# Self-attention in three float32r products: rows of v's two forms 320 floats apart, and the projection's tiles in the attention's buffers

## The chip, the cores and the metric

The kernel runs on one core of a Trainium2 chip. The metric is the device time of one execution in microseconds (us), the median of three runs. The engines are TensorE (PE; its weight loads are listed apart as PEld), VectorE (DVE), ScalarE (ACT), GpSimd (POOL) and SyncE (SP), which issues transfers.

## The reference, cut to what matters

```python
# x: (4, 64, 64, 256) float32; Wq, Wk: (256, 128); Wv: (256, 256); gamma: (1,)
q = einsum('bwhc,cd->bwhd', x, Wq) + bq          # N = 64*64 = 4096
k = einsum('bwhc,cd->bwhd', x, Wk) + bk
v = einsum('bwhc,cd->bwhd', x, Wv) + bv
pq, pk, pv = (t.reshape(B, -1, N) for t in (q, k, v))   # (4, 128, N), (4, 128, N), (4, 256, N)
energy = einsum('bcn,bcm->bnm', pq, pk)
attention = softmax(energy, axis=-1)
out = einsum('bcm,bnm->bcn', pv, attention)
return gamma * out.reshape(x.shape) + x
```

Four images, each with 4096 x 4096 energies over a depth of 128, and a sum over them with 256 rows of v.

## The kernel before: the parts that are touched

[...] The kernel therefore splits each operand into forms and adds up three products: for the energies two into `sa` and one into `sb`, for the attention `h` with `vh` and `l` with `vl` into one sum and `d` with `vd` into another. An image is handled in 16 groups of 256 queries; a group has 8 steps of 512 keys (4 tiles of 128). In each step TensorE does 12 energy products and 24 attention products. In a product the first operand named below is the stationary one, of 128 x 128, loaded as weights; the second one streams past, 256 or 258 columns of it. Two extra columns of ones in `vh` and `vl` give the sums that softmax divides by.

```python
NB = 256; NJ = NB // P; NG = N // NB; NU = NM // 4; STEPS = NG * NU; LOOK = 3
VC = C + 4                                   # floats in a row of vh and vl: 260
# ... pools in order of place:
xpool, xtpool, qkv = pool("xpool", 3), pool("xtpool", 3), pool("qkv", 1)
pool("pad", 1).tile([P, 16], F32, name="pad")
ppool = pool("ppool", 2)
pool("pad2", 1).tile([P, 112], F32, name="pad2")
work, kpool = pool("work", 2), pool("kpool", 3)
# ...
vh = qkv.tile([P, NM, VC], F32R, tag="vh", name="vh")
vl = qkv.tile([P, NM, VC], F32R, tag="vl", name="vl")
vd = qkv.tile([P, NM, C], F32R, tag="vd", name="vd")
# ... energies of half a step:
for i in range(2):
    for to, f, first, last in ((sa, 0, True, False), (sa, 1, False, True), (sb, 2, True, True)):
        nc.tensor.matmul(to[:, i], kt[:, 2 * k + i, f, :], q[:, f], start=first, stop=last)
# ... attention products of a step; h, l and d are ppool tiles [P, 4, NB]:
for left, right in ((h, vh), (l, vl), (d, vd)):
    for j in range(NJ):
        out_ = bb[:, j, :] if left is d else acc[j]
        for i in range(4):
            m = 2 * t + i // 2 + NI * (i % 2)
            nc.tensor.matmul(
                out_, left[:, i, j * P : (j + 1) * P], right[:, m, : out_.shape[1]],
                # ... start, stop
            )
```

Before an image's attention comes its projection, 16 iterations of 256 tokens: x is transposed, and TensorE computes q and k (`qk`) and v; q and the forms of k go to DRAM and come back tile by tile. The energies of the first steps are mixed into its last iterations (`begin`), and the first tiles of the next image are projected within the last steps of an image.

```python
def qk_out(i):
    now["qk"] = work.tile([P, 2, 2 * C2], F32, tag="qk", name=f"qks_{b}_{i}")
    return ((now["qk"], 0),)
def v_out(i):
    now["v4"] = work.tile([P, KC, C], F32, tag="v4", name=f"v4_{b}_{i}")
    return now["v4"], bv4_sb, 1.0 / E
# ... in project_qk:
f = kpool.tile([P, 2, 3, P], F32R, tag="f", name=f"f_{b}_{i}", bufs=2)
halved(f, x[:, :, C2:])
nc.gpsimd.dma_start(kf[b, i // 2][:, i % 2], f.rearrange("p s j d -> p s (j d)"))
# ...
def load_q(b, g):
    t = work.tile([P, NJ, P], F32, tag="qr", name=f"qr_{b}_{g}", bufs=1)
    nc.sync.dma_start(t, qd[b, g])
    loads[b, "qr", g] = t
# ... the loop of an image's steps, cut:
for u in range(STEPS):
    # ... energies of step u + 3; join and upper (x*y and h) of step u + 2
    halves(b, u + 1)          # l and d of the next step
    attend(b, u)
    # ... at a group's end: whole, finish (scale, transpose, add x, store)
```

Of the kernel before, what the change touches and what calls it, by code (L numbers as in the profile page):

```python
# [9 lines left out]
F32 = mybir.dt.float32  # L10
F32R = mybir.dt.float32r
# [9 lines left out]
def kernel(  # L21
# [37 lines left out]
    B, W, H, C = x.shape  # L59
    P = 128  # L60
    N = W * H
    C2 = C // 2
    NM = N // P
    KC = C // P
# [10 lines left out]
    XB = 256  # L75
# [98 lines left out]
    NB = 256  # L174
    NJ = NB // P
# [1 line left out]
    NU = NM // 4  # L177
    STEPS = NG * NU
    LOOK = 3
    VC = C + 4  # L180
    E = 2.0**-12


# [15 lines left out]
    with ExitStack() as fast:  # L199
        fast.enter_context(tc.manual_schedule())  # L200
        pool = lambda name, bufs, **kw: fast.enter_context(
            tc.tile_pool(name=name, bufs=bufs, **kw)
        )
        xpool, xtpool, qkv = pool("xpool", 3), pool("xtpool", 3), pool("qkv", 1)

        pool("pad", 1).tile([P, 16], F32, name="pad")
        ppool = pool("ppool", 2)
        pool("pad2", 1).tile([P, 112], F32, name="pad2")
        work, kpool = pool("work", 2), pool("kpool", 3)
        dram = pool("dram", 2, space=DRAM)  # L210
        ps_s = pool("ps_s", 2, space=PSUM)
# [3 lines left out]
# [4 lines that stand above are left out]
# [3 lines left out]
        images, qd, kf, units, loads, now = [], {}, {}, {}, {}, {}  # L222
# [14 lines left out]
        def image(b):  # L237
            def xt_out(i):
                return xtpool.tile([P, KC, 2, P], F32, tag="xt", name=f"xts_{b}_{i}")

            def qk_out(i):
                now["qk"] = work.tile([P, 2, 2 * C2], F32, tag="qk", name=f"qks_{b}_{i}")
                return ((now["qk"], 0),)

            def v_out(i):
                now["v4"] = work.tile([P, KC, C], F32, tag="v4", name=f"v4_{b}_{i}")
                return now["v4"], bv4_sb, 1.0 / E

            images.append(Projection(b, xpool, lambda: next(now["banks"]), xt_out, qk_out, v_out))

            for g in range(NG):
                qd[b, g] = dram.tile([P, NJ, P], F32, tag=f"qd{g}", name=f"qd_{b}_{g}")
            for t in range(NU):
                kf[b, t] = dram.tile([P, 2, 2, 3 * P], F32R, tag=f"kf{t}", name=f"kf_{b}_{t}")

        def halved(f, x):

            h = f[:, :, 0, :]
            nc.scalar.activation(h, x, AF.Identity, scale=UPPER / 64)
            for j, s, op in ((1, -64.0, ALU.add), (2, 64.0 * (1.0 + E), ALU.subtract)):  # L260
                nc.vector.scalar_tensor_tensor(
                    f[:, :, j, :], h.bitcast(F32), s, x, ALU.mult, op
                )

        def project_qk(b, i):
            images[b].qk(i)
            x = now["qk"]
            for s in range(2):
                nc.gpsimd.dma_start(qd[b, i // 2 + NG // 2 * s][:, i % 2, :], x[:, s, :C2])
            f = kpool.tile([P, 2, 3, P], F32R, tag="f", name=f"f_{b}_{i}", bufs=2)  # L270
            halved(f, x[:, :, C2:])
            nc.gpsimd.dma_start(kf[b, i // 2][:, i % 2], f.rearrange("p s j d -> p s (j d)"))

# [15 lines left out]
                )  # L289

        def load_q(b, g):
            t = work.tile([P, NJ, P], F32, tag="qr", name=f"qr_{b}_{g}", bufs=1)
            nc.sync.dma_start(t, qd[b, g])
            loads[b, "qr", g] = t

        def halve_q(b, g):
            t = work.tile([P, 3, NJ, P], F32R, tag="q", name=f"q_{b}_{g}")
            halved(t.rearrange("p f j d -> p j f d"), loads.pop((b, "qr", g)))
            loads[b, "q", g] = t

        def load_k(b, u):
            if u < STEPS:
                t = kpool.tile([P, 4, 3, P], F32R, tag="k", name=f"k_{b}_{u}")
                nc.gpsimd.dma_start(t.rearrange("p (i s) f d -> p i s (f d)", s=2), kf[b, u % NU])  # L304
                loads[b, "k", u] = t

        def energy(b, u, k):

            g, t = divmod(u, NU)
            if k == 0:  # L310
                x = ppool.tile([P, 4, NB], F32, tag="x", name=f"x_{b}_{u}", bufs=3)
                y = ppool.tile([P, 4, NB], F32, tag="y", name=f"y_{b}_{u}")
                units[b, u] = x, y
            x, y = units[b, u]
            q, kt = loads[b, "q", g], loads[b, "k", u]
            sa = ps_s.tile([P, 2, NJ, P], F32, tag="a", name=f"sa_{b}_{u}_{k}")
            sb = ps_s.tile([P, 2, NJ, P], F32, tag="b", name=f"sb_{b}_{u}_{k}")
# [3 lines that stand above are left out]
                        to[:, i], kt[:, 2 * k + i, f, :], q[:, f], start=first, stop=last  # L321
                    )
            for to, sp, scale in ((x, sa, (1.0 + E) / E), (y, sb, -1.0 / E)):
                nc.scalar.activation(  # L324
                    to[:, 2 * k : 2 * k + 2, :],
                    sp.rearrange("p i j d -> p i (j d)"),
                    AF.Exp,
                    scale=scale,
                )

        def join(b, u):

            x, y = units[b, u]
            nc.vector.tensor_tensor(x, x, y, ALU.mult)  # L334
            units[b, u] = x

        def upper(b, u):
            h = ppool.tile([P, 4, NB], F32R, tag="h", name=f"h_{b}_{u}", bufs=3)
            nc.scalar.activation(h, units[b, u], AF.Identity, scale=UPPER)  # L339
            units[b, u] = units[b, u], h  # L340
# [123 lines left out]

        def begin(b, i):

            if i == 5:
                load_q(b, 0)
            if i == 9:
                halve_q(b, 0)  # L470
            if i in (4, 6, 8):
                load_k(b, i // 2 - 2)
            if i >= 10:
                energy(b, (i - 10) // 2, i % 2)
            if i in (12, 14):
                join(b, i // 2 - 6)
            if i in (13, 15):
                upper(b, i // 2 - 6)
                load_k(b, i // 2 - 3)

        image(0)
        for b in range(B):
            pr = images[b]
            if b == 0:
                now["banks"] = energies
                pr.transposed(0)
                pr.transposed(1)
                project_qk(b, 0)
            for i in range(1, NI):
                if i == 3:  # L490
                    now["banks"] = outputs
                if i + 1 < NI:
                    pr.transposed(i + 1)
                while i == 1 and active:
                    proceed()
                begin(b, i)
                project_qk(b, i)
                if i == NI - 1:
                    halves(b, 0)
                project_v(b, i - 1)  # L500
                proceed()
            project_v(b, NI - 1)
            for u in range(STEPS):
                g, t = divmod(u, NU)
                ahead = u + LOOK
                if ahead // NU + 1 < NG and ahead % NU == 3:
                    load_q(b, ahead // NU + 1)
# [32 lines left out]
            if b + 1 < B:  # L540
                images[b + 1].transposed(1)
                project_qk(b + 1, 0)

    NB = 512
    NG = N // NB
    NJ = NB // P
    NP = NM // 2
    xg, og = columns(x, NB), columns(out, NB)
    with tc.If(nc.values_load(again[0:1, 0:1]) > 0), ExitStack() as general:
        pool = lambda name, bufs, **kw: general.enter_context(  # L550
            tc.tile_pool(name=name, bufs=bufs, **kw)
        )
        xpool, xtpool, qkv = pool("gx", 2), pool("gxt", 2), pool("gqkv", 1)
        ppool, work = pool("gp", NP + 2), pool("gw", 1)
# [3 lines left out]
        for b in range(B):  # L558
# [16 lines left out]
            for g in range(NG):  # L575
                ps = []
                mx = work.tile([P, 2, NB], F32, tag="mx", name=f"gmx_{b}_{g}")
                for t in range(NP):
# [9 lines left out]
                    p = ppool.tile([P, 2, NB], F32, tag="p", name=f"gp_{b}_{g}_{t}")  # L588
# [89 lines left out]
```

## Time and profile before

| | before |
|---|---|
| time, median of 3 runs | 2481.36 us (2479.54 to 2482.91) |
| span of the profiled execution | 2476.8 us |
| TensorE busy | 2463.2 us (99%), 19,982 records |
| weight loads busy | 2419.1 us (98%) |
| VectorE / ScalarE / GpSimd busy | 2103.2 (85%) / 1807.9 (73%) / 424.4 us (17%) |
| granted TensorE clock | 0.999 |
| energy products `sa`, `sb` | 4096 and 2048 |
| attention products h, l, d | 4096 each |
| projection products `qk`, `v` (records) | 512 each, 121.3 and 120.3 us busy |

A line of the costliest groups reads: line, engine, operation, output <- inputs, shape, count, then busy time and the mean of one in ns, then the idle time of the engine before them and who ended it. Two of VectorE's and one of ScalarE's:

```profile
L334 DVE TENSOR_TENSOR x<-x,y 128x1024 f32<-128x1024 f32 x512 | 625.8, 1222 | 144.2 <-ACT y L324 144.2
L345 DVE TENSOR_TENSOR l<-x,h 128x1024 fp32r<-128x1024 f32 x512 | 624.2, 1219 | 0.0
L339 ACT ACTIVATE h<-x 128x1024 fp32r<-128x1024 f32 x512 | 543.6, 1062 | 46.3 <-DVE x L334 38.4
```

Products overlap in TensorE's pipeline, so the duration of one (276 ns and more) is over twice the distance between the starts of two; the time is made by that distance. The last part of the page has the transfers, with the median time from issue to landing:

```profile
x<-in_x_dram SPq DMA_DIRECT2D x128, 256.0 KB, 4.3
kf<-f POOLq DMA_DIRECT2D x64, 384.0 KB, 3.7
...
qd<-qks POOLq DMA_DIRECT2D x128, 64.0 KB, 3.1
qr<-qd SPq DMA_DIRECT2D x64, 128.0 KB, 3.0
```

### The profile page before, as it was taken

The page shows a single profiled execution, that of the slowest core. Times are in us where ns is not written, and L with a number is a line of the kernel's source. Part 1 is how long each engine was busy: PE and PEld are TensorE (multiplying, and loading weights), DVE is VectorE, ACT ScalarE, POOL GpSimd, SP SyncE. Part 2 cuts the span into 40 slices and gives each one's busy share as a digit, 9 for nine tenths or more (in the row PEclk, how much of TensorE's full clock was granted, in tenths as well). Part 3 has the DMA queues.
Part 4 walks back from the last instruction along what each step waited for, and adds up shares of the span by engine and source line. Part 5 has one row for each costly group of instructions (what it writes and reads, how often), then busy time and mean ns, then how long its engine had stood idle before and what let it go on. Part 6 is the DMA issues. An engine that isn't in the chain of part 4 may idle for free.

```text
span 2476.8 us, 50085 instructions
## 1 busy us (share of the span) xinstructions
PE 2463.2 (99%) x19982; PEld 2419.1 (98%) x19982; DVE 2103.2 (85%) x2440; ACT 1807.9 (73%) x3138; POOL 424.4 (17%) x780
## 2 busy tenths in 40 slices
PE   9999999999999999999999999999999999999998
PEld 8999999999899999999989999999998999999998
DVE  5888888888698888888869888888886988888887
ACT  5777777777677777777667777777766777777775
POOL 4211111111411111111141111111114111111110
PEclk9999999999999999999999999999999999999999
DMA  7766666674766666666477666666647666666663
GB/s 235 218 194 213 202 206 200 196 217 150 236 215 195 207 202 207 203 193 215 138 239 224 199 195 209 205 209 196 199 146 247 219 202 198 204 204 209 200 201 110
DMA packets 137408, 498.92 MB, mean 201 GB/s; under 512 B 15536, under 2 KB 57264, under 8 KB 137168
## 3 DMA queue, kind: packets, MB, share of 16 engines
q0 software_dynamic: 92320, 453.17, 58.4%
q1 hardware_dynamic: 44304, 42.22, 5.7%
q8 instruction: 160, 2.62, 0.4%
q14 instruction: 80, 0.66, 0.1%
q10 hardware_dynamic: 544, 0.26, 0.0%
HBM read 445.25 MB, written 50.33 MB: 200 GB/s over the span
## 4 chain that ended last, share of the span: by engine, by line
PE 95%; ACT 2%; DVE 1%; issue 1%; DMA 1%; POOL 0%; SPq 0%; ACTq 0%; DVEq 0%; POOLq 0%
PE a L370 39%; PE bb L370 19%; PE sa L320 18%; PE sb L320 10%; PE qk L136 4%; PE v L157 4%; PE ot L416 1%; PE xt L123 1%; ACT h L339 1%; DVE x L334 1%; ACT x L324 0%; ACT y L324 0%; ACT vh L284 0%; DVE vd L287 0%; DMA kf<-f 0%
## 5 line engine op out<-in xcount | busy, mean ns | idle before, releaser
L324 ACT ACTIVATE x<-sa 128x512 f32<-128x512 f32 x1024 | 607.5, 593 | 381.0 <-PE sa L320 334.9
L334 DVE TENSOR_TENSOR x<-x,y 128x1024 f32<-128x1024 f32 x512 | 625.8, 1222 | 144.2 <-ACT y L324 144.2
L320 PE MATMUL sa<-q,k 128*128 128x256 f32 x4096 | 740.2, 279 | 1.2 <-ACT x L324 1.1
L345 DVE TENSOR_TENSOR l<-x,h 128x1024 fp32r<-128x1024 f32 x512 | 624.2, 1219 | 0.0
L348 DVE SCALAR_TENSOR_TENSOR d<-h,x 128x1024 fp32r<-128x1024 f32 x512 | 624.1, 1219 | 0.0
L320 PEld LDWEIGHTS sa<-q,k 128*128 128x128 f32 x4096 | 619.9, 188 | 2.6 <-ACT x L324 1.9
L324 ACT ACTIVATE y<-sb 128x512 f32<-128x512 f32 x1024 | 613.3, 599 | 0.0
L370 PE MATMUL a<-vh,h 128*128 128x258 f32 x4096 | 579.8, 284 | 0.0
L339 ACT ACTIVATE h<-x 128x1024 fp32r<-128x1024 f32 x512 | 543.6, 1062 | 46.3 <-DVE x L334 38.4
L320 PE MATMUL sb<-q,k 128*128 128x256 f32 x2048 | 574.3, 280 | 0.0
L370 PE MATMUL a<-vl,l 128*128 128x258 f32 x4096 | 573.8, 282 | 0.0
L370 PE MATMUL bb<-vd,d 128*128 128x256 f32 x4096 | 557.2, 278 | 0.0
L304 POOL DMA_DIRECT2D k<-kf x512 | 279.6, 546 | 1468.0 <-PE sb L320 1449.5
L370 PEld LDWEIGHTS a<-vh,h 128*128 128x128 f32 x4096 | 523.9, 189 | 2.2
L370 PEld LDWEIGHTS a<-vl,l 128*128 128x128 f32 x4096 | 525.7, 189 | 0.0
L370 PEld LDWEIGHTS bb<-vd,d 128*128 128x128 f32 x4096 | 514.7, 188 | 0.0
L320 PEld LDWEIGHTS sb<-q,k 128*128 128x128 f32 x2048 | 384.7, 188 | 9.0 <-ACT y L324 0.8
L400 DVE SCALAR_TENSOR_TENSOR o<-a,o 128x256 f32<-128x256 f32 x126 | 47.6, 420 | 87.0 <-ACT o L380 87.0
L136 PE MATMUL qk<-wqk_sb,xts 128*128 128x256 f32 x512 | 121.3, 380 | 0.0
L157 PE MATMUL v<-xts,wv_sb 128*128 128x256 f32 x512 | 120.3, 379 | 0.0
L157 PEld LDWEIGHTS v<-xts,wv_sb 128*128 128x128 f32 x512 | 97.3, 190 | 13.2
L408 ACT ACTIVATE o<-o,r 128x256 f32<-128x256 f32 x126 | 57.2, 501 | 72.5 <-DVE r L391 72.5
(54 smaller groups left out, 928.5 us busy)
## 6 DMA issues: line engine op xcount, KB each, us to landing
k<-kf POOLq DMA_DIRECT2D x512, 768.0 KB, 4.7
x<-in_x_dram SPq DMA_DIRECT2D x128, 256.0 KB, 4.3
kf<-f POOLq DMA_DIRECT2D x64, 384.0 KB, 3.7
out_dram<-x POOLq DMA_DIRECT2D x63, 256.0 KB, 2.6
qd<-qks POOLq DMA_DIRECT2D x128, 64.0 KB, 3.1
qr<-qd SPq DMA_DIRECT2D x64, 128.0 KB, 3.0
wv_sb<-in_L_conv_Wv_dram POOLq DMA_DIRECT2D x1, 256.0 KB, 5.5
out_dram<-x SPq DMA_DIRECT2D x1, 256.0 KB, 4.2
```

The lines of the kernel that those rows point to most:

```text
L136: nc.tensor.matmul(qk[:, s, :], self.xt[i][:, k, s, :], wqk_sb[:, k, :], start=(k == 0), stop=(k == KC - 1),)
L157: nc.tensor.matmul(vp[:, eh, :], wv_sb[:, k, eh * P : (eh + 1) * P], self.xt[i][:, k].rearrange("p s a -> p (s a)"), start=(k == 0), stop= ...
L304: nc.gpsimd.dma_start(t.rearrange("p (i s) f d -> p i s (f d)", s=2), kf[b, u % NU])
L320: nc.tensor.matmul(to[:, i], kt[:, 2 * k + i, f, :], q[:, f], start=first, stop=last)
L324: nc.scalar.activation(to[:, 2 * k : 2 * k + 2, :], sp.rearrange("p i j d -> p i (j d)"), AF.Exp, scale=scale,)
L334: nc.vector.tensor_tensor(x, x, y, ALU.mult)
L339: nc.scalar.activation(h, units[b, u], AF.Identity, scale=UPPER)
L345: nc.vector.tensor_tensor(l, x, h.bitcast(F32), ALU.subtract)
L348: nc.vector.scalar_tensor_tensor(d, h.bitcast(F32), 1.0 + E, x, ALU.mult, ALU.subtract)
L370: nc.tensor.matmul(out_, left[:, i, j * P : (j + 1) * P], right[:, m, : out_.shape[1]], start=(t == i == 0 and (left is h or left is d and ...
L400: nc.vector.scalar_tensor_tensor(o[:, j, :], a[:, :C], 1.0 + E, o[:, j, :], ALU.mult, ALU.add)
L408: nc.scalar.activation(o[:, j, :], o[:, j, :], AF.Identity, scale=r[:, j : j + 1])
```

## The change

Each product reads two operands in each partition of the on-chip memory (SBUF) at the same time: the streaming one and the next weights. Rows of `vh` and `vl` are 260 floats, 1040 bytes, apart, so that the distance between the two addresses, modulo 256, goes through all multiples of 16 from row to row. The change makes a row 320 floats, 1280 bytes, so that this distance is 64 bytes modulo 256 in every product of the attention, as it already is for `vd` and for the energies. The longer rows take 15,360 bytes more in each partition. Room for that comes from the projection: its tiles `qk`, `f`, `v4` and `qr` move from buffers of their own into those that the attention uses for `d`, `l`, `o` and x. Since `qr` now lies in one of the three buffers of x, its first load in an image comes at iteration 8 in place of 5. A smaller pad keeps the later pools at the addresses that the 64 bytes ask for.

```diff
-    VC = C + 4
+    VC = C + 64
@@ pools
-        pool("pad2", 1).tile([P, 112], F32, name="pad2")
+        pool("pad2", 1).tile([P, 48], F32, name="pad2")
@@ qk_out, v_out
-                now["qk"] = work.tile([P, 2, 2 * C2], F32, tag="qk", name=f"qks_{b}_{i}")
+                t = ppool.tile([P, 2, 4 * C2], F32, tag="d", name=f"qks_{b}_{i}")
+                now["qk"] = t.rearrange("p s c -> p (s c)")[:, : 4 * C2]
+                now["qk"] = now["qk"].rearrange("p (s c) -> p s c", s=2)
-                now["v4"] = work.tile([P, KC, C], F32, tag="v4", name=f"v4_{b}_{i}")
+                now["v4"] = work.tile([P, KC, C], F32, tag="o", name=f"v4_{b}_{i}")
@@ project_qk
-            f = kpool.tile([P, 2, 3, P], F32R, tag="f", name=f"f_{b}_{i}", bufs=2)
+            f = ppool.tile([P, 4, NB], F32R, tag="l", name=f"f_{b}_{i}")
+            f = f.rearrange("p i n -> p (i n)")[:, : 6 * P]
+            f = f.rearrange("p (s j d) -> p s j d", s=2, j=3)
@@ load_q
-            t = work.tile([P, NJ, P], F32, tag="qr", name=f"qr_{b}_{g}", bufs=1)
+            t = xpool.tile([P, 2, XB], F32, tag="x", name=f"qr_{b}_{g}")[:, 0, :]
+            t = t.rearrange("p (j d) -> p j d", j=NJ)
@@ begin
-            if i == 5:
+            if i == 8:
                 load_q(b, 0)
```

## The prediction

> **What bounds the kernel now.** I read the page first: which engine is full, and what the chain that ended last consists of.
>
> ```profile
> PE 2463.2 (99%) x19982; PEld 2419.1 (98%) x19982; DVE 2103.2 (85%) x2440; ACT 1807.9 (73%) x3138; POOL 424.4 (17%) x780
> ...
> PE 95%; ACT 2%; DVE 1%; issue 1%; DMA 1%; POOL 0%; SPq 0%; ACTq 0%; DVEq 0%; POOLq 0%
> PE a L370 39%; PE bb L370 19%; PE sa L320 18%; PE sb L320 10%; PE qk L136 4%; PE v L157 4%; PE ot L416 1%; PE xt L123 1%; ACT h L339 1%; DVE x L334 1%; ACT x L324 0%; ACT y L324 0%; ACT vh L284 0%; DVE vd L287 0%; DMA kf<-f 0%
> ```
>
> TensorE is the chain, and its granted clock is full in all 40 slices. Nothing can be won beside it; the question is how fast one product follows another. A busy matrix engine says nothing of that, so I went next to the durations by tile, of the h, l and d products and of the two energies:
>
> ```profile
> L370 PE MATMUL a<-vh,h x4096: 276/283/367, 74.7 to 2464.3; 128*128 128x258 f32 x196
> ...
> L370 PE MATMUL a<-vl,l x4096: 276/283/290, 75.6 to 2465.2; 128*128 128x258 f32 x196
> ...
> L370 PE MATMUL bb<-vd,d x4096: 275/277/286, 76.6 to 2466.2; 128*128 128x256 f32 x196
> ...
> L320 PE MATMUL sa<-q,k x4096: 276/276/469, 44.7 to 2454.7; 128*128 128x256 f32 x196
> ...
> L320 PE MATMUL sb<-q,k x2048: 276/276/388, 45.0 to 2454.8; 128*128 128x256 f32 x187
> ```
>
> The three numbers are minimum, median and maximum in ns. All five kinds have the same minimum, so 258 columns against 256 don't explain the rest: energies sit on their minimum, d products 1 to 2 ns above, and h and l products 7 ns. The chain of one query group, in order of time, then gives the pace itself (start, length):
>
> ```profile
> 1413.80 1.93 PE a L370 x16
> 1415.73 0.91 PE bb L370 x8
> 1416.64 0.23 PE sa L320 x2
> ...
> 1418.00 1.91 PE a L370 x16
> 1419.91 0.92 PE bb L370 x8
> 1420.83 0.23 PE sa L320 x2
> ...
> 1424.10 0.95 PE bb L370 x8
> 1425.05 0.23 PE sa L320 x2
> ...
> 1426.46 1.91 PE a L370 x16
> ```
>
> From 1416.64 to 1418.00 run 12 energy products: 1.36/12 = 113.3 ns each. The 16 h and l products take 1.91/16 = 119.4, the 8 d products 0.91 to 0.92, or 114 to 115. One step in this group, from 1425.05, has its energies at 1.41/12 = 117.5, with the same addresses as elsewhere: there seem to be two steady paces, 113.3 and 117.5. A last look, at engine time in the five groups from 1400 us, says whether the others would let TensorE go faster:
>
> ```profile
> 1400.00:1572.33 172.33, 172.33 (x1462) 171.48 (x1461) 150.92 (x166) 129.60 (x221) 24.76 (x45) 1.00 0.65 203
> ```
>
> TensorE, weight loads, VectorE, ScalarE, GpSimd in that order: VectorE is at 88%, ScalarE at 75%.
>
> **What the Trainium skill says.** "TensorE: Matmul & The Clock Gate", section "Back-to-back issue gap", gives N/2.4 + 2.5 ns, so an estimate of 109.2 ns for 256 columns and 110.0 for 258; its section "LDWEIGHTS (loading the stationary operand)" gives columns/1.2, so 106.7 ns for 128. Every product here has a new weight tile, so a load and a product run side by side all the time; the trace's floor is 113.3, some 4 ns above either. "SBUF — State Buffer", section "Who interferes with whom", gives TensorE two independent read ports and says that PE never waits on anyone. The trace disagrees: equal shapes at equal clock last 276 to 290 ns, depending on which tile they read. Its 16-byte lines (section "Door 1: The DMA port swizzle") don't separate the cases either: rows of 1040 and of 1280 bytes both start on a line. So no page states the effect that this change is after; the trace carries it alone.
>
> **The change part by part.** I added up the tile sizes of the pools in order, each rounded up to 32 bytes. Before: h, l, d and k start at 96 modulo 256, vd and q at 32. d products and energies thus read operands 64 bytes apart, every row alike. vh starts at 32 too, but its rows are 1040 bytes = 4 x 256 + 16 apart, so the distance takes all 16 multiples of 16 in turn. vl is the same. After: rows are 1280 = 5 x 256 bytes apart, and all rows of vh and vl sit at 32. vh and vl grow by 2 x 7680 = 15,360 bytes. The dropped work tiles (qk 4096, v4 4096, qr 1024, f 6144) and 256 of the pad give 15,616. Summing again, ppool starts at 96, q is at 32, k at 96: every attention product has -64.
>
> 1. h and l products. In the chain of the whole group from 1400.40 to 1434.86 us, the eight pieces of 16 sum to 15.46 us, less about 0.11 for the one stall: 15.35/128 = 119.9 ns. Seven stretches of 12 energies sum to 6 x 1.36 + 1.41 = 9.57 us, or 113.9 ns, both paces mixed. Two more columns add at most 113.3 x 2/256 = 0.9. New pace, an estimate from these: 114.8. Saved: 8192 x 5.1 ns = 42 us, all on the chain.
> 2. d products. The eight pieces sum to 7.41 us: 115.8 ns. After energies they'd be 113.9; the excess is, I think, the first few after the last l product, before the steady pace comes back. With l in step, I take 114.3: 4096 x 1.5 ns = 6 us.
> 3. Energies: 6144 products, already at 113.9; 0.
> 4. Group ends. The piece of 2.04 and the transposes' stretch (1411.76 to 1413.80, 2.04 less 0.44 and 1.36 = 0.24) hold 0.13 + 0.24 = 0.37 us of waiting per group, 24 us in all; it comes from ScalarE's and VectorE's work at the group's end and stays. With a group at 33.7 us, VectorE's 30.2 is 90%: a little more waiting, say 2 us lost.
> 5. Projection: its products read wqk_sb with xts and xts with wv_sb, whose addresses don't change. The page has 121.3 and 120.3 us for them over 64 iterations: 3.8 us an iteration, four images' worth untouched.
> 6. The tiles moved to other buffers: qk now shares the ring of d (two), f that of l (two), v4 that of o (two); each had two before. Counts per image are even, so a tile meets the same slot as before one image on. At the image's end the first qk tile takes the buffer of the last d but one, done before its product even starts. qr takes one of three x buffers at iteration 8 and is halved at 9: the buffer's last reader is the transpose in iteration 7, so there are two iterations, 7.7 us, for a load of 3.0 us. At i = 15 and just after it, halves waits for the stores of qk and f two tiles back (3.1 and 3.7 us to landing) in at most 2 us of TensorE's time per image; with its look-ahead of three steps I expect 0 to 4 us in all.
>
> Sum: 42 + 6 - 2 - 2 = 44 us saved, 2437 us, if the 64 bytes do for h and l what they do for d and energies.
>
> **The rivals.**
> - Modulo 512 or more. In before all the good pairs are also -64 modulo 512, so the trace cannot tell 256 from 512. Rows of 1280 bytes alternate by 256 modulo 512, and in each step two of four h products have an odd row. If those stay at 120 and keep disturbing the rest, only a third or so is won: about 2463.
> - The slow pace catches on. Energies after 1425.05 keep 117.5 until an h product breaks the pattern. With all products in step nothing breaks it but the group's end. If half of the products go at 117.5, the mean is 115.4 over 18,432 products against 116.9 now (with 119.9, 115.8 and 113.9): 28 us, so 2453. If none do, 113.3 (114.2 for h and l) everywhere gives 47 + 10 + 4 = 61 us: 2420.
> - It is not the addresses but VectorE and ScalarE, which read and write in SBUF meanwhile, or the 258 columns: then nothing changes, 2481. Against it: d and l products of a step have the same neighbours and differ by 4 to 5 ns; the minima are equal.
> - The shared buffers cost a wait in the projection: a few us per image, 2485 to 2490 together with no gain. The ring counts speak against it.
>
> **Range and chances.** I give the plain version 0.6 (2420 to 2453), the modulus 0.25 (2463), no effect 0.1, a loss 0.05. The middle is near 2440. 2% is 49.6 us, under 2431.7: only where h and l go at 114 and the slow pace stays rare, 0.3.
>
> **What would show it.** Medians of vh and vl products at 276 to 278 in place of 283; pieces of 16 at 1.83 to 1.85 us; bb pieces at 0.91; group period near 33.8. Medians of 280 or more, or durations that alternate with the row, would speak for the modulus; energies at 117.5 in more than one step of eight for the slow pace; a new wait of VectorE for a store, for the buffers. I am wrong if vh's median stays at 283.
>
> Predicted time 2440 us, range 2418 to 2474; faster by over 2% 0.3, within 2% 0.66, slower by over 2% 0.04.

## The result, and the profile after

The changed kernel takes 2486.76 us (median of 4 runs, 2484.73 to 2489.42) where the kernel before takes 2480.67 us (2479.54 to 2482.91) beside it: a ratio of 1.0024, 95% interval 1.0007 to 1.0041. It is slower by some 6 us, and the 40 us that were expected didn't come. Runs below are given as ratios to the kernel before on the same chip, since its own median goes from 2481 to 2485 us from chip to chip.

The engines' busy times hardly move. This is the first part of the page after; its part on the chain is empty in this profile, so the order of time has to serve.

```profile
PE 2469.3 (99%) x19982; PEld 2423.4 (98%) x19982; DVE 2103.4 (85%) x2440; ACT 1805.3 (73%) x3138; POOL 424.4 (17%) x780
```

The durations by tile after (minimum, median and maximum in ns):

```profile
L375 PE MATMUL a<-vh,h x4096: 277/283/370, 74.2 to 2471.8; 128*128 128x258 f32 x196
...
L375 PE MATMUL a<-vl,l x4096: 280/283/289, 75.2 to 2472.8; 128*128 128x258 f32 x196
...
L375 PE MATMUL bb<-vd,d x4096: 276/277/286, 76.2 to 2473.7; 128*128 128x256 f32 x196
```

The medians of h and l are still 283. What did change is the minimum of l: 280 in place of 276. With mixed distances 15% of the l products are followed by the next start within less than 116 ns; now none is. TensorE's instructions in order of time (start, length, then what) show one step after another:

```profile
1421.85 0.40 PE L325 MATMUL sa<-q,k 128*128 128x256 f32 x2
...
1423.26 1.12 PE L375 MATMUL a<-vh,h 128*128 128x258 f32 x8
1424.22 1.12 PE L375 MATMUL a<-vl,l 128*128 128x258 f32 x8
1425.18 1.09 PE L375 MATMUL bb<-vd,d 128*128 128x256 f32 x8
1426.10 0.39 PE L325 MATMUL sa<-q,k 128*128 128x256 f32 x2
...
1427.46 1.12 PE L375 MATMUL a<-vh,h 128*128 128x258 f32 x8
```

16 h and l products take 1425.18 - 1423.26 = 1.92 us, 120.0 ns each. The 12 energies go at 1.36/12 = 113.3 from 1426.10, and at 1.41/12 = 117.5 from 1421.85: the two paces of before are still there. Third, the waits after (waiting engine and line, who ended it, us in total, times, longest) have an entry that before doesn't have, and one that grew from 1.0 us:

```profile
ACT x L329 <- DVE d L353: 7.0, 8, 2.4
...
DVE l L350 <- DMA kf<-f: 4.6, 4, 2.0
```

VectorE waits once in each image for the store of f out of the buffer that l now needs.

The pace of each kind, the mean distance between the starts of two products, can be worked out from the start times in the trace. I leave out distances of 140 ns and more, and sum these up as waits: what each is over 114 ns. All kernels of this study, in ns (float32r is the type of the h, l, d and energy products in all of them); those with 256 or 248 columns in both h and l, and the one with rows of 256, form no sums for softmax:

| kernel | columns of h, l | h | l | d | energies | waits, us | ratio (95%) |
|---|---|---|---|---|---|---|---|
| before | 258 | 120.0 | 119.8 | 115.7 | 114.3 | 33 | 1 |
| after | 258 | 120.3 | 120.7 | 115.4 | 114.2 | 38 | 1.0024 (1.0007 to 1.0041) |
| buffers alone | 258 | 119.7 | 119.7 | 116.0 | 114.8 | 39 | 1.0021 (1.0013 to 1.0028) |
| rows 320 | 256 | 114.1 | 114.1 | 114.2 | 114.2 | 43 | 0.9785 (0.9769 to 0.9802) |
| rows 260 | 256 | 118.4 | 118.0 | 115.7 | 114.2 | 35 | 0.9931 (0.9914 to 0.9947) |
| rows 256 | 258 | 120.4 | 120.8 | 114.9 | 113.7 | 38 | 0.9999 (0.9990 to 1.0008) |
| rows 320 | 248 | 114.7 | 115.0 | 116.7 | 115.9 | 38 | 0.9908 (0.9893 to 0.9923) |
| rows 320 | 264 | 123.3 | 120.1 | 116.5 | 113.7 | 37 | 1.0075 (1.0060 to 1.0091) |
| rows 320 | 272 | 123.9 | 123.3 | 117.8 | 117.7 | 29 | 1.0199 (1.0182 to 1.0216) |
| distances 0, +128 | 256 | 117.8 | 119.2 | 116.3 | 113.7 | 41 | 0.9982 (0.9975 to 0.9990) |
| distances 0, +128 | 258 | 120.4 | 120.9 | 118.0 | 116.5 | 33 | 1.0104 (1.0087 to 1.0121) |
| rows 320, ones in h | 258, 256 | 120.4 | 115.1 | 113.9 | 114.1 | 39 | 0.9929 (0.9914 to 0.9944) |
| old buffers, ones in h | 258, 256 | 120.0 | 116.0 | 114.5 | 114.9 | 37 | 0.9952 (0.9939 to 0.9966) |
| rows 320 and 256, ones in h | 258, 256 | 120.4 | 115.2 | 114.0 | 114.1 | 37 | 0.9896 (0.9879 to 0.9912) |

The energies have two paces, 113.3 and 117.5 ns, and in before it is not chance which one they take. There the energies that follow the fourth step of a group start 117.8 ns apart in each of the 64 groups, and those after the third, the sixth and the seventh step 113.2 to 113.3 ns apart in each of the 64. The energies' own tiles lie alike modulo 256 in all steps, so I take it that the attention products ahead of them decide, which read other rows in each step. The stretch from 1425.05 us that the prediction shows is one that follows a fourth step. In after the pattern is less strict: after the second step 41 of the 64 stretches are slow, after the third 19, after the fourth 2.

The table closes for before and after: 4096 x (0.3 + 0.9 - 0.3) ns = 3.7 us, the energies -0.6, the waits 4 to 5, together 7 to 8; the two spans differ by 2484.4 - 2476.8 = 7.6 us.

### The profile page after: what moved, and what is told of

It reads as the page before. It is cut to its first block, busy times and chain, and to the rows that moved or that the text cites. A ratio compares the mean times of both kernels' runs of the same rounds, so it can differ in the third digit from the quotient of the medians.

```text
span 2484.4 us, 50133 instructions
## 1 busy us (share of the span) xinstructions
PE 2469.3 (99%) x19982; PEld 2423.4 (98%) x19982; DVE 2103.4 (85%) x2440; ACT 1805.3 (73%) x3138; POOL 424.4 (17%) x780
## 4 chain that ended last, share of the span: by engine, by line
## 5 line engine op out<-in xcount | busy, mean ns | idle before, releaser
L136 PE MATMUL qk<-wqk_sb,xts 128*128 128x256 f32 x512 | 121.3, 380 | 0.0
L157 PE MATMUL v<-xts,wv_sb 128*128 128x256 f32 x512 | 120.3, 379 | 0.0
```

Source lines behind the costliest of these rows:

```text
L136: nc.tensor.matmul(qk[:, s, :], self.xt[i][:, k, s, :], wqk_sb[:, k, :], start=(k == 0), stop=(k == KC - 1),)
L157: nc.tensor.matmul(vp[:, eh, :], wv_sb[:, k, eh * P : (eh + 1) * P], self.xt[i][:, k].rearrange("p s a -> p (s a)"), start=(k == 0), stop= ...
```

## The experiments

After the result there were two theories. Width: 258 columns cost a whole stretch more than 256, wherever the rows lie. Modulus: the distance must agree modulo 512 or more, which rows of 1280 bytes don't give.

### Rows of 320 floats, h and l products of 256 columns

```diff
-                    out_ = bb[:, j, :] if left is d else acc[j]
+                    out_ = bb[:, j, :] if left is d else acc[j][:, :256]
```

The two columns of ones are left out of the products, and 1 stands for softmax's sums.

> The changed kernel with h and l products of 256 columns in place of 258. The two columns of ones are left out of the products, so the sums that softmax divides by are not formed (1 is used); everything else runs. Width theory (258 columns cost a whole extra stretch of about 16 columns, whatever the rows): h and l products fall from about 120.5 ns to about 114 ns apart, 8192 x 6.5 = 53 us saved, time 2430 to 2440 us, median duration of vh and vl products 276 to 278. Modulus theory (the distance of the two operands must agree modulo 512 or more, and rows of 1280 bytes alternate by 256): h and l stay at 118 to 121 ns, time 2475 to 2487 us.

0.9785 (0.9769 to 0.9802): 2432.02 us, 53 us under the kernel before. By tile:

```profile
L375 PE MATMUL a<-vh,h x4096: 276/276/369, 75.2 to 2420.1; 128*128 128x256 f32 x196
...
L375 PE MATMUL a<-vl,l x4096: 276/276/281, 76.2 to 2421.1; 128*128 128x256 f32 x196
```

Medians of 276: h and l are where the energies are. The order of time shows a step that goes in one pace:

```profile
1422.64 1.07 PE L375 MATMUL a<-vh,h 128*128 128x256 f32 x8
1423.54 1.07 PE L375 MATMUL a<-vl,l 128*128 128x256 f32 x8
1424.45 1.07 PE L375 MATMUL bb<-vd,d 128*128 128x256 f32 x8
1425.36 0.39 PE L325 MATMUL sa<-q,k 128*128 128x256 f32 x2
...
1426.72 1.07 PE L375 MATMUL a<-vh,h 128*128 128x256 f32 x8
```

The step lasts 1426.72 - 1422.64 = 4.08 us, or 36 products of 113.3 ns. The modulus theory falls here too: rows of 1280 bytes alternate by 256 modulo 512, and the products on odd rows are as fast as those on even ones.

### Rows of 260 floats, 256 columns

The same edit in the kernel before; the sums are left out as above.

> The kernel before (rows of 260 floats) with h and l products of 256 columns, sums left out as in the run on 320 floats. If the width alone sets the pace, the rows don't matter: 2425 to 2435 us, like its twin. If both matter (width and address distance), it stays above its twin: h and l at 117 to 119 ns, 2455 to 2475 us. If only the addresses matter, it stays at 2470 to 2481 us and the twin as well or not.

0.9931 (0.9914 to 0.9947), the middle answer. By tile:

```profile
L370 PE MATMUL a<-vh,h x4096: 273/281/368, 78.5 to 2455.6; 128*128 128x256 f32 x196
...
L370 PE MATMUL a<-vl,l x4096: 275/281/288, 79.4 to 2456.5; 128*128 128x256 f32 x196
```

With 256 columns the rows matter: medians of 281 ns on rows 1040 bytes apart, 276 on rows 1280 apart. Leaving out the columns alone has won something too: h and l go from 120 to 118 ns, and the time falls by 0.7%, 17 us. Its twin has the shared buffers as well, which cost 0.2% (below), so the even distance is worth 0.9931 - 0.9785 + 0.002 = 1.7%, some 41 us. This is the gain that the change was made for, and it exists; with 258 columns it is 0 within the noise, as after less buffers alone is 0.0003.

### Rows of 256 floats, 258 columns

```diff
-    VC = C + 64
+    VC = C
@@ attend: the streaming operand of h and l, over the row's end
+    (vhx if left is h else vlx)[:, m * C : m * C + C + 2]
```

The last two columns are the next row's first two; no sums are formed.

> The changed kernel with rows of 256 floats, so that all operands of h, l, d are 64 bytes apart modulo 1024 as for d, and with 258 columns: the last two are the first two of the next row, so no sums are formed (1 is used). Width theory: h and l stay at 120 to 121 ns, time 2478 to 2490 us. Modulus theory (512 or more): they fall to 114 to 115 ns, time 2430 to 2445 us.

0.9999 (0.9990 to 1.0008). The agreement is less than I expected. By the tile sizes h's operands are 64 bytes apart modulo 512 in every row, and l's modulo 256 only, since each of the two tiles is 33,024 bytes long; modulo 1024 the weights themselves lie 512 bytes apart. Still, the finer agreement of h does nothing for 258 columns: h goes at 120.4, l at 120.8.

### 272, 264 and 248 columns

```diff
-            nc.scalar.copy(t[:, :, C : C + 2], ones...)
+            nc.scalar.copy(t[:, m0 : m0 + 8, C : C + 16], ones...)   # 272; 264 likewise; acc as wide
```

With 272 and 264 nothing is left out. With 248 the sums and 8 of the 256 channels are left out of the h and l products.

> The changed kernel with h and l products of 272 columns (16 of ones in place of 2), nothing left out. Width theory in steps of 16 columns: 272 costs what 258 does, h and l stay near 120 to 121 ns, time within 8 us of 2487. If width counts column by column: 14 columns [...] are 6 ns more, 8192 x 6 = 49 us, 2530 to 2540 us. Modulus theory says nothing of it.

> The changed kernel with h and l products of 264 columns (8 of ones), nothing left out. If any width over 256 costs the same until a next multiple of 16 is passed: h and l at 120 to 121 ns, about 2487 us. If the columns count one by one: [...]2.5 ns more than with 258, 2505 to 2510 us. If it falls into the slow pace altogether as 272 columns did (energies and d at 117.5 ns), 2520 us or more.

> The changed kernel with h and l products of 248 columns: the sums and 8 of 256 channels are left out of them. If a width that isn't a multiple of 16 columns (64 bytes) loses the steady pace: h and l at 116 to 121 ns, slower than with 256 columns, 2445 to 2487 us. If fewer columns simply take less time: at or below 113.5 ns, 2425 to 2432 us.

272 columns: 1.0199, 2534.30 us. The time lies in the range expected for columns that count one by one, but that is luck: h and l lost half of the 6 ns, and the rest came from products that weren't widened. Against the changed kernel h and l lost 3.6 and 2.6 ns, 25 us together; d and the energies, whose instructions are the same, lost 2.4 and 3.5, 31 us more. (The waits are 9 us less.) By tile:

```profile
L375 PE MATMUL bb<-vd,d x4096: 278/281/283, 79.7 to 2523.1; 128*128 128x256 f32 x196
...
L325 PE MATMUL sa<-q,k x4096: 276/281/469, 47.8 to 2511.3; 128*128 128x256 f32 x196
```

Their medians went from 276 or 277 to 281: 95% of the energies start 116 ns or more apart, so they run at the slow pace nearly from one end of a group to the other. This is the slow pace catching on, which the prediction had as a rival for the change itself. 264 columns: 1.0075, 2499.34 us, between the expected answers, so that none of them came true. l is at a constant 120 ns, h at 123.3, and the energies are at the fast pace. So the pace of d and the energies doesn't simply follow the number of columns of the products before them; what in those products decides wasn't tried.

248 columns: 0.9908, slower than 256 (0.9785) with 3% fewer columns in 8192 products; the spans are 2457.0 and 2432.7 us, 24 us apart. The order of time shows where:

```profile
1420.74 1.07 PE L375 MATMUL a<-vh,h 128*128 128x248 f32 x8
1421.64 1.07 PE L375 MATMUL a<-vl,l 128*128 128x248 f32 x8
1422.55 1.10 PE L375 MATMUL bb<-vd,d 128*128 128x256 f32 x8
1423.49 0.40 PE L325 MATMUL sa<-q,k 128*128 128x256 f32 x2
...
1424.90 1.09 PE L375 MATMUL a<-vh,h 128*128 128x248 f32 x8
1425.83 1.10 PE L375 MATMUL a<-vl,l 128*128 128x248 f32 x8
```

Here h and l take (1422.55 - 1420.74)/16 = 113.1 ns, hardly less than the 113.3 of 256 columns. I take it that something other than the columns sets 113, perhaps the weight load beside each product, which is the same in all runs; that isn't shown. Then d and the energies go at 0.94/8 and 1.41/12 = 117.5, and the next h at (1425.83 - 1424.90)/8 = 116.3. I had expected h and l themselves to leave the pace; mostly d and the energies after them do, and the energies by turns: in the mean over the groups they go at 117.3 to 117.7 after the second, fourth, sixth and eighth step, and at 113.9 to 114.1 after the third, fifth and seventh.

### Other distances

```diff
+        qkv.tile([P, 16], F32, tag="p0", name="p0")      # ahead of vh: 64 bytes
+        qkv.tile([P, 32], F32, tag="p1", name="p1")      # ahead of vl: 128 more
+        qkv.tile([P, 16], F32, tag="p2", name="p2")      # ahead of vd: back to -64
```

> The changed kernel with h and l products of 256 columns (sums left out), rows of 320 floats, and vh and vl at other distances from their weights: h 0 and l +128 bytes modulo 256, d and the energies at -64 as they are. If -64 is what makes 113 to 114 ns: h and l at 117 to 121 ns each, time 2455 to 2480 us. If any constant distance does (it is the change of distance from row to row that costs): 2430 to 2440 us, like the run of 320 floats and 256 columns.

With 256 columns (sums left out), 0.9982 (0.9975 to 0.9990): a constant distance isn't enough. By tile:

```profile
L378 PE MATMUL a<-vh,h x4096: 274/281/362, 78.4 to 2463.6; 128*128 128x256 f32 x196
...
L378 PE MATMUL a<-vl,l x4096: 274/281/287, 79.3 to 2464.6; 128*128 128x256 f32 x196
```

At 0 the h products go at 117.8, at +128 the l products at 119.2, where -64 gives 114.1. All 16 multiples of 16 mixed gave 118.4 and 118.0. So -64 is a good place among those tried; -32 or -96 weren't tried alone, and h and l were moved together, so that each may have spoiled the other's pace. Nor is -64 enough for a product by itself. On rows of 260 floats the first step of a group has its rows at -64 and -48: h goes at 119.4 there, against 116.3 in the first step on rows of 320.

One rival stands untested. By the tile sizes the weights start at 96 modulo 256 in every kernel here, and only the streaming rows were moved. The runs therefore can't tell the distance of the two operands from the address of the streaming one alone. Where this text speaks of distance, it may be that address.

> The changed kernel, nothing left out (258 columns, rows of 320 floats), with vh 0 and vl +128 bytes from their weights modulo 256 in place of -64. If 258 columns cost [...] at any distance (the width alone): h and l at 120 to 121 ns, time within 5 us of 2487. If 258 columns have a good distance of their own and one of these two is near it: that product at 114 to 117 ns, 2460 to 2475 us. If -64 still helps 258 columns a little: h or l at 122 to 124 ns, 2495 to 2510 us.

With 258 columns and nothing left out, 1.0104 (1.0087 to 1.0121). h and l go at 120.4 and 120.9, as at -64, as the width theory says; but its time is missed by 20 us, because 70% of the energies, and d with them, fell into the slow pace:

```profile
L378 PE MATMUL bb<-vd,d x4096: 276/281/287, 79.2 to 2496.7; 128*128 128x256 f32 x196
...
L328 PE MATMUL sa<-q,k x4096: 276/281/469, 47.3 to 2485.1; 128*128 128x256 f32 x196
```

### The buffers alone

```diff
-    VC = C + 64
+    VC = C + 4
```

> The second half of the change alone: the projection's tiles in the attention's buffers, rows of 260 floats as before. By the start times of the changed kernel's products, about 4 us of its loss are waits of TensorE, all at an image's beginning, and about 4 us the h and l products' pace. If that reading holds: 2482 to 2486 us where the kernel before has 2481, and VectorE waits for a store of f as in the changed kernel. If the buffers cost nothing: equal to the kernel before within 2 us.

1.0021 (1.0013 to 1.0028), 5 us. It has the waits of the changed kernel:

```profile
ACT x L329 <- DVE d L353: 5.8, 7, 2.2
...
DVE l L350 <- DMA kf<-f: 4.5, 4, 1.9
```

The halves of the image's first steps wait for f's store, and with them what stands behind d. TensorE's waits within 15 us of an image's first h product sum to 2.0 us in before, 5.9 in after and 6.0 here. The buffers alone are as slow as the whole change; the rows add nothing.

### Columns of ones in h alone

Without the two columns the changed kernel gets 1.0024 - 0.9785 = 2.4% faster, some 59 us, so I looked for a way to have fewer of them. l is the small rest of p, the exponentials, after h. The kernels below take softmax's sums from h alone. The first simply leaves out the low parts; the others divide h's sum by 1 - 2^-13, the factor that h was made with, and leave out only the low parts' spread about their mean. That is a less exact sum than both kernels form.

```diff
-                    out_ = bb[:, j, :] if left is d else acc[j]
+                    out_ = bb[:, j, :] if left is d else acc[j] if left is h else acc[j][:, :C]
```

> The changed kernel with the columns of ones in the h products alone; l products have 256 columns, and the low parts are left out of softmax's sums. Width theory, product by product: half of the 54 us, with a few products after the h ones still out of step: 2455 to 2465 us; h near 120 ns, l near 115 ns. If one kind of wide product keeps the whole step out of pace: above 2470 us.

In the changed kernel: 0.9929 (0.9914 to 0.9944), 2463 us. h stays at 120.4, l falls to 115.1. The first four l products after the wide ones go at 118, 117, 116 and 114 ns in the mean, then the pace is back.

> The kernel before with all its buffers, but columns of ones in vh alone and rows of vl of 256 floats, so that l products have 256 columns at -64 bytes. Softmax's sums take h alone and are divided by 1 - 2^-13 (one constant), so they leave out the low parts' spread about their mean. From the pace of l 119.8 to 115.1 ns and of d 115.7 to 113.9 ns as in the changed kernel with ones in h alone: 4096 x 4.7 + 4096 x 1.8 = 27 us saved, 2454 us; that run less what the shared buffers cost there, 2463 - 5 = 2458, says the same. If the rows of 260 of vh keep l and d out of pace: 2465 to 2475 us.

In the kernel before, with rows of vl of 256 floats: 0.9952, 2469 us, 10 to 15 us above the first answers, and in the range of the other one: rows of 260 floats in vh keep l and d out of pace. It happens in the same steps of nearly every group. d goes at 117.7 in the second and third step and at 113.3 to 113.9 in the others, and the energies after these two steps are at 117.7 in 63 of 64 groups.

> Rows of vh 320 floats, of vl 256, columns of ones in vh alone, so that all operands are 64 bytes apart modulo 256 and l and d products have 256 columns; of the shared buffers only those of qk and v4 (f, qr and the load at iteration 5 stay as before). Softmax's sums take h alone, divided by 1 - 2^-13. If the even distance after the wide h products is what the run on the old rows lacked, and the waits of the shared buffers are f's: 2463 - 4 = 2459 us, 2456 to 2462, with energies and d at 113.9 to 114.2 ns. If the slow pace is drawn at random: 2464 to 2470 us. If the shared qk tile makes the waits: 2463 us.

Rows of vh of 320, of vl of 256, f and qr back in buffers of their own: 0.9896 (0.9879 to 0.9912), 2459.19 us against 2485.29 beside it, faster than both kernels by 1%. l and d have the pace of the first of the three, and VectorE's wait for f's store is gone; TensorE's waits around an image's start are down to 2.7 us:

```profile
L372 PE MATMUL a<-vl,l x4096: 276/277/286, 76.5 to 2444.7; 128*128 128x256 f32 x196
...
L372 PE MATMUL bb<-vd,d x4096: 276/276/283, 77.4 to 2445.6; 128*128 128x256 f32 x196
```

## Why the prediction was wrong

**The step that failed** is the first of the change, and before it the reading that led there: "All five kinds have the same minimum, so 258 columns against 256 don't explain the rest", and "Two more columns add at most 113.3 x 2/256 = 0.9". A minimum over 4096 products is the luckiest one; it says what a product can take once, not what a run of them takes. The other argument against the width, that d and l have the same neighbours and differ by 4 to 5 ns, compared 256 columns with 258. At an even distance the two columns cost 120.5 - 114.1 = 6.4 ns, seven times what I allowed, and they alone hold h and l at 120 (rows of 256, 260 and 320 floats, distances mixed, -64, 0 and +128: 119.7 to 120.9). The formula of the Trainium skill ("TensorE: Matmul & The Clock Gate", "Back-to-back issue gap") is linear in the columns like mine, but the page gives it for the isolated gap and says that in a stream of weight loads and products both set the spacing. For this stream it doesn't hold: on rows of 320 floats 248, 256, 258, 264 and 272 columns take 114.8, 114.1, 120.5, 121.7 and 123.6 ns.

Three smaller readings of the prediction were off. The floor of 113.3 is 4 ns above the formula's 109.2 but 6.6 above 106.7, and the weight loads are recorded at a mean of 188 to 189 ns. "Equal shapes at equal clock" holds within l, 276 to 290 ns, but h and l have 258 columns and d and the energies 256, so the medians of different tiles don't show that the tile's place matters, and don't disagree with what the prediction cites of two independent read ports. The runs with 256 columns do show that the place matters (114.1 against 118), and not whether the ports are the reason. And the mean pace before is 117.0 by its terms, not 116.9.

**The effect is there for 256 columns.** Rows at a constant -64 bytes are worth 41 us there against the 48 predicted, and the pace reached is the one of the energies, as I had argued. With 258 columns they are worth nothing: the columns alone hold h and l at 120. The mixed rows alone hold them at 118. From 120, leaving out the columns alone wins 17 us, evening the rows alone nothing, and both together 53 us. A profile of before can't show that; the experiment with both removed does. Whether it is the distance, as the prediction has it, or the address of the streaming rows stays open.

**d products**: predicted 114.3, "with l in step". l didn't get in step, and d stayed at 115.4. The excess lies where the prediction guessed: in after, the first three of eight d products go at 118.1, 117.7 and 116.3 ns, the next four at 114. With 256 columns in l they go at 113.9 to 114.5 (where l is at -64), so this step hung on the first.

**Energies, projection, group ends** stayed as predicted (energies 114.2 against 113.9; the page after has 121.3 and 120.3 us for the projection's products, as before; the waits at groups' ends are there in every run).

**Buffers**: predicted 0 to 4 us; 5 us measured (3 to 7), some 4 of them waits of TensorE at the images' starts, where VectorE waits as the prediction said, for a store of f two tiles back. With f and qr in buffers of their own these waits are nearly gone.

**The rivals.** Modulus 512: refuted by the run on 320 floats with 256 columns, and for h also by rows of 256. The slow pace catching on: not in the changed kernel (by the start times a fifth of its energies are at 116 ns or more, as in before), but most of all in three variants: with 272 columns 95%, with 258 at distances 0 and +128 70%, with 248 58%. "The 258 columns: then nothing changes" stood in half a sentence beside VectorE and ScalarE and had a share of the 0.1 for no effect; it is the one that came true.

## What to carry to other kernels

Judge the cost of a product's shape by the pace of a long run of such products, not by the shortest one. When two conditions must hold together for a good pace, an edit that meets one may show little or nothing, so try both at once, with a part left out if need be, before building the layout for one. For dense float32r products, 256 columns with the operands at addresses that were measured to be good are worth having: here two columns more for a sum cost 6.4 ns, 6% of a product.

## What the runs showed of the hardware that I had not expected

Fewer columns can be slower: 248 against 256 cost 24 us in a span of 2433. There are two steady paces for equal float32r products of 256 columns at equal addresses, 113.3 and 117.5 ns, and a run of products tends to keep the one it falls into. In before the choice repeats from group to group: all 64 stretches of energies after a fourth step are slow. Products of 258 columns go at about 120 ns (119.7 to 120.9) in all places tried for their operands (mixed, -64, 0 and +128 bytes). With the two operands 64 bytes apart in every row, products of 256 columns reach 113.3; with h at 0 and l at +128 bytes they take 117.8 and 119.2. What in the memory or in the matrix engine does this stays open: the trace shows starts and ends, not reads, and I only argue that the weight load and the product that run side by side get in each other's way.
